# A macaron block on one core: one batch of weighted sums per sequence, a fourth buffer of exponentials, feed-forward products in place

## The chip, the cores and the metric

The kernel runs on one core of a Trainium2 chip. The metric is the device time of one execution in microseconds (us). The core's engines run side by side: PE (TensorE, matrix products, with its weight loads shown as PEld), DVE (VectorE), ACT (ScalarE), POOL (GpSimd) and SP (SyncE, which issues most transfers).

## The reference, cut to what matters

Sixteen sequences of 256 tokens with 256 features pass through half a feed-forward layer, an attention layer and the same half feed-forward layer again, each behind a layer norm and added to its input.

```python
x = x + 0.5 * ffn(layernorm(x))      # silu(x Wu) * (x Wg), times Wd; 1024 hidden features
x = x + attention(layernorm(x))      # 16 heads of 16, keys and values in 4 groups, causal
x = x + 0.5 * ffn(layernorm(x))      # weights quantised to -s, 0, s with s = mean |W|

# of the attention, per sequence and head
scores = where(causal, -inf, q @ k.T / sqrt(16))
attn = softmax(scores, axis=-1)      # over the keys
out = attn @ v                       # the sums over the keys
```

## The kernel before, in words

The 16 sequences are handled in eight blocks n of two (512 tokens). The feed-forward layer is cut into *units*: a unit (ffn_unit, L464) makes 128 of the 1024 hidden features for a block, by four matmuls u and four g of 512 columns (products, L448), and each block has eight units per pass, so that there are 128 in all. After a unit ACT makes th of the u product and DVE makes h: for the first four keys of `order` (SILU = 4) with a Silu and one DVE product (L480, L481), for the other twelve with a Tanh (L483), a DVE product th+1 times u into a tile tmp (L485) and a DVE product with g (L486). ACT then rounds h to 16 bits (L491) and POOL keeps the remainder (L492). Four ffn_down steps (L496) take the products back to 256 features by 16 matmuls d each (L502), and DVE adds them to x (L507).

Before that the three weight matrices are quantised at the start: ternary_sums (L277) adds up absolute values on ACT, with the mapped values going to a tile junk that nothing reads, and on DVE; ternary_piece (L312) then makes each quarter of a matrix in two steps, a tile dn (values under the lower bound; on ACT, DVE or POOL) and the DVE product of L321 that reads dn and writes tu, tg or td.

The attention of sequence q (n, s = divmod(q, 2)) goes through these steps: project and values (queries, keys, values of the block, matmuls qkv), load (transfers of Qs and ks), peak and peak_parts (largest score of each row, DVE L625 and L635 to L646), peak_rows (transposes pt, ACT copy, and a transfer into Qs), exponents, weighted and attended:

- exponents(q, g), L663: for group g three score matmuls st of 512 columns (L675), three ACT exponentials into a tile pT (L676), and two POOL selects that put zeros above the diagonal (L684; issued one step later).
- weighted(q, gp), L693: for the two groups 2gp and 2gp+1 the sums over the keys. Each matmul (L706) has 128 keys and 32 columns of weights (16 values and a one for the denominator) and writes a quarter of the partitions, so four heads' matmuls stand side by side in the array. A first half of the keys goes with 256 query columns, the second with 128. Each group has a PSUM bank of its own, half used, and ACT copies each group's [128, 256] into a tile oT (L713). There are 16 matmul calls in a weighted; the profile shows each as two instructions, since the numbers are 32-bit, so 32 for a call.
- attended(q, gp), L716: four transposes ot, a reciprocal and a product on DVE, and an addition to x on POOL (L733).

Tiles come from pools with a number of slots per tag: pT has 3 slots, oT 3, tmp 3 (the products of L485 and the dn pieces), th 3 (th and junk), and PSUM has 8 banks. A tile that finds no free slot waits until a former one's last reader is done.

Three things set the order of the work. A planner in the kernel (Step, run) issues steps from six chains: the feed-forward chain, and the chains of the norms, loads, sequences, peaks and projections. A step has a cost in planner's microseconds and lags after earlier steps: weighted costs 1.64 and follows LAG_PROB = 3.0 after the second exponents it needs, attended 1.2 after weighted. The sequence chain issues one sequence's steps as e0, e1, e2, w0, e3, a0, w1, a1, with the next sequence's e0 put ahead of w1 (L881 to L888). Attention steps that are due go first, as long as they are not ahead of the feed-forward chain by PACE. The tile library then orders each engine's instructions by its own simulated timeline (L1098); pin (L223) keeps a batch's matmuls in their written order among themselves.

Steps that wait for exponentials by name: load(q) for exponents(q-3, 3) (L839), peak(q, 0) for exponents(q-2, 3) (L849), and the attention's norm of block n for weighted(2(n-3)+1, 1) (L822).

Of the kernel before, what the change touches and what calls it, by code (L numbers as in the profile page):

```python
# [97 lines left out]
def macaron_kernel(  # L98
# [83 lines left out]
    wg = raw[1].rearrange("p (c f) -> p c f", c=EC)  # L182
    wd = raw[2].rearrange("p (c e) -> p c e", c=FC)
    QS = [r.bitcast(F16).rearrange("p (t h q) -> p t h q", t=2, h=H) for r in raw]
    wqkv = ap_.tile([P, 3, 512], F32, tag="pT", name="wqkv", bufs=3)[:, :EC, : 3 * P]

    def load_x(n):
        nc.sync.dma_start(xs[n], x_t[n])
# [49 lines left out]
    def constant_rows():  # L238


        c = ap_.tile([P, 2, 1536], F16, tag="pT", name="constant_rows", bufs=3)
        k, v = c[:, 0, : 3 * S], c[:, 1, :P]
        nc.gpsimd.memset(k[KP:KR], 0.0)
        ku = k[KP:KR].rearrange("p (v u k) -> p v u k", v=3, k=U)
        for which, base in ((EVEN, 0), (ODD, 32)):
            nc.gpsimd.affine_select(
                out=ku[:, which], in_=ku[:, which], pattern=[[0, S // U], [-1, U]],
                compare_op=ALU.is_ge, fill=-MASK, base=base, channel_multiplier=1,
            )
        nc.gpsimd.memset(k[KR : KR + 3], -MROW)  # L250
        nc.gpsimd.memset(v[KP:KR], 0.0)
        vj = v[KP:KR].rearrange("p (j b) -> p j b", b=4)
        nc.gpsimd.affine_select(
            out=vj, in_=vj, pattern=[[1, 32], [0, 4]], compare_op=ALU.not_equal,
            fill=MASK, base=0, channel_multiplier=-1,
        )
        for to in Ks:
            nc.sync.dma_start(
                to[KP : KR + 3].rearrange("p g v k -> p g (v k)"),
                k[KP : KR + 3].unsqueeze(1).to_broadcast([KR + 3 - KP, G, 3 * S]),  # L260
            )
        box["queries"] = v
# [48 lines left out]

    def ternary_piece(wi, ti, hi, lo, name):  # L312
        engine = {"u": ENG_U, "g": ENG_G, "d": ENG_D}[name[0]][int(name[1])]
        dn = fp.tile([P] + list(wi.shape[1:]), BF16, tag="tmp", name=f"dn_{name}")
        if engine == "a":
            nc.scalar.activation(dn, wi, AF.Relu, bias=lo, scale=-1.0)
            nc.scalar.activation(dn, dn, AF.Sign)
        else:
            by = nc.gpsimd if engine == "p" else nc.vector
            pin(PINT and engine == "v", by.tensor_scalar(dn, wi, lo, None, ALU.is_lt))  # L320
        nc.vector.scalar_tensor_tensor(ti, wi, hi, dn, ALU.is_gt, ALU.subtract)  # L321
# [142 lines left out]
    def ffn_unit(key, f):  # L464
        n, p = key
        name = f"{p}_{n}_{f}"
        if f == 0:
            hidden[key] = hp.tile([P, FC, 2, 512], F16, tag="hT", name=f"hT_{p}_{n}")
        hT = hidden[key]
        if (key, f) not in half_done:  # L470
            ffn_up(key, f)
        up = half_done.pop((key, f))
        gate = bank([P, 512], f"g_{name}")
        if key == order[0] and f < 6:
            warm(int(NWF[f]), f"g{f}")
        products(key, f, tg, gate)
        th = fp.tile([P, 512], F32, tag="th", name=f"th_{name}")
        h = fp.tile([P, 512], F32, tag="h", name=f"h_{name}")
        if key in order[:SILU]:
            nc.scalar.activation(th, up, AF.Silu, scale=scales["one_u"])  # L480
            nc.vector.scalar_tensor_tensor(h, gate, scales["per_u"], th, ALU.mult, ALU.mult)  # L481
        else:
            nc.scalar.activation(th, up, AF.Tanh, scale=scales["half_u"])  # L483
            tmp = fp.tile([P, 512], F32, tag="tmp", name=f"tmp_{name}")
            nc.vector.scalar_tensor_tensor(tmp, th, 1.0, up, ALU.add, ALU.mult)  # L485
            nc.vector.scalar_tensor_tensor(  # L486
                h, gate, 0.25 / (NORM * NORM), tmp, ALU.mult, ALU.mult
            )

        def split():  # L490
            nc.scalar.copy(hT[:, f, 0, :], h)  # L491
            nc.gpsimd.tensor_tensor(hT[:, f, 1, :], h, hT[:, f, 0, :], ALU.subtract)  # L492

        later(1, urgent(HP_FFN, split))
# [168 lines left out]
    def exponents(q, g):  # L663
        n, s = divmod(q, 2)
        Qs, ks = made[n][s], Ks[q % NBUF]
        pT = ap_.tile([P, 3, 512], F32, tag="pT", name=f"pT_{q}_{g}", bufs=3)
        probs[q, g] = pT
        every = slice(0, KR + 3)
        for u in range(3):
            sc = bank([P, 512], f"st_{q}_{g}_{u}")  # L670
            if u < 2:
                keys, mov = ks[every, g, PLAIN, 0:P], Qs[every, u, 4 * g : 4 * g + 4, :]
            else:
                keys, mov = ks[every, g, PLAIN, P:], Qs[every, 1, 4 * g : 4 * g + 4, :]
            nc.tensor.matmul(sc, keys, mov, start=True, stop=True)  # L675
            nc.scalar.activation(  # L676
                pT[:, u, :].rearrange("p (h b j) -> p h b j", h=4, b=4),
                sc.rearrange("p (h j b) -> p h b j", h=4, b=4), AF.Exp, scale=exp_scale,
            )

        def causal():
            for u in (0, 2):
                v = pT[:, u, :].rearrange("p (h t) -> p h t", h=4)
                nc.gpsimd.affine_select(  # L684
                    out=v, in_=v, pattern=[[0, 4], [1, P]], compare_op=ALU.is_ge,
                    fill=0.0, base=0, channel_multiplier=-1,
                )

        later(1, urgent(HP_CAUSAL, causal))

    sums = {}

    def weighted(q, gp):  # L693

        n, s = divmod(q, 2)
        v = VT[n % NVAL]
        groups = (2 * gp, 2 * gp + 1)
        pT = [probs.pop((q, g)) for g in groups]
        o = [bank([P, S], f"o_{q}_{g}") for g in groups]
        first = True  # L700
        for half in range(2):
            for i2, g in enumerate(groups):
                for i in range(4):
                    at = o[i2][32 * i : 32 * i + 32]
                    moving = pT[i2][:, 2 * half : 2, i * P : (i + 1) * P] if half == 0 else pT[i2][:, 2, i * P : (i + 1) * P]
                    pin(not first, nc.tensor.matmul(  # L706
                        at[:, half * P :], v[:, 2 * s + half, g, :], moving,
                        start=half == 0, stop=half == 1, tile_position=(0, 32 * i),
                    ))
                    first = False  # L710
        for i2, g in enumerate(groups):
            oT = ap_.tile([P, S], F32, tag="oT", name=f"oT_{q}_{g}", bufs=3)
            nc.scalar.copy(oT, o[i2])  # L713
            sums[q, g] = oT

    def attended(q, gp):  # L716
        n, s = divmod(q, 2)
        ot = bank([P, 2, 2 * P], f"ot_{q}_{gp}").rearrange("p b (h d) -> p b h d", d=32)
        for gg in range(2):
            oT = sums.pop((q, 2 * gp + gg))  # L720
            for b in range(2):
                nc.tensor.transpose(  # L722
                    ot[:, b, 4 * gg : 4 * gg + 4, :].rearrange("p h d -> p (h d)"),
                    oT[:, b * P : (b + 1) * P], ident,
                )
        rs = small.tile([P, 2, 8, 1], F32, tag="rs", name=f"rs_{q}_{gp}")
        nc.vector.reciprocal(rs, ot[:, :, :, D : D + 1])
# [83 lines left out]
    def qkv_chain():  # L811
        steps = []
        for n in range(NSB):
# [5 lines left out]
            if n > 1:  # L819
                need.append((("load", 2 * n - 3), 0.0))  # L820
            if n >= NVAL:
                need.append((("weighted", 2 * (n - NVAL) + 1, 1), 0.0))  # L822
            at = 8 * n - QKV_LEAD
            if at >= 0:
                need.append((("exponents", at // 4, at % 4), 0.0))
# [36 lines left out]
    def sequence_chain():  # L862
        steps = []
        for q in range(2 * NSB):
            e = [
                Step(0.66, lambda q=q, g=g: exponents(q, g), ("exponents", q, g),
                     [(("exponents", q, g - 1), GAP_EXP)] if g else
                     [(("rows", q), LAG_MAX), (("values", q // 2), 0.0)])
                for g in range(4)
            ]  # L870
            w = [
                Step(1.64, lambda q=q, gp=gp: weighted(q, gp), ("weighted", q, gp),
                     [(("exponents", q, 2 * gp + 1), LAG_PROB)])
                for gp in range(2)
            ]
            a = [
                Step(0.43, lambda q=q, h=h: attended(q, h), ("attended", q, h),
                     [(("weighted", q, h), 1.2)])
                for h in range(2)
            ]  # L880
            steps.append([e[0], e[1], e[2], w[0], e[3], a[0], w[1], a[1]])  # L881
        flat = []
        for q, mine in enumerate(steps):
            flat += mine

        for q in range(1, 2 * NSB):
            i = 8 * q
            flat[i - 2 : i + 1] = [flat[i], flat[i - 2], flat[i - 1]]  # L888
        return flat

# [211 lines left out]
```

## Time and profile before

| | |
|---|---|
| three runs, median | 563.08 us (561.78 to 563.2) |
| the profiled execution, its own time | 560.4 us |
| its span, first to last instruction | 558.7 us |
| mean granted clock of TensorE | 0.991 |
| weighted sums, matmuls o (L706) | 1024 instructions, 49.4 us busy |
| copies of the sums (L713) | 64 of 128x256, 388 ns each |
| exponentials (L676) | 192, 697 ns each |
| selects (L684) | 128, 636 ns each |
| th (L483), its product (L485), h (L486) | 96 each, 692, 683 and 685 ns |

The profile is of one execution. "Busy" is the time in which at least one instruction of a group ran on its engine; a matmul's end is modelled, so matmuls in a row overlap by their records, and the distance of two starts says more than a duration. In a list of groups, `out<-in` gives the tiles by the program's names, then partitions x elements, and the idle time of the engine in front with what ended it. In a timeline neighbouring instructions of a kind are merged, with their number behind x. In a list of waits the three numbers are the sum, how often, and the longest.

### The profile page before, as it was taken

The page shows a single profiled execution, that of the slowest core. Times are in us where ns is not written, and L with a number is a line of the kernel's source. Part 1 is how long each engine was busy: PE and PEld are TensorE (multiplying, and loading weights), DVE is VectorE, ACT ScalarE, POOL GpSimd, SP SyncE. Part 2 cuts the span into 40 slices and gives each one's busy share as a digit, 9 for nine tenths or more (in the row PEclk, how much of TensorE's full clock was granted, in tenths as well). Part 3 has the DMA queues.
Part 4 walks back from the last instruction along what each step waited for, and adds up shares of the span by engine and source line. Part 5 has one row for each costly group of instructions (what it writes and reads, how often), then busy time and mean ns, then how long its engine had stood idle before and what let it go on. Part 6 is the DMA issues. An engine that isn't in the chain of part 4 may idle for free.

```text
span 558.7 us, 12132 instructions
## 1 busy us (share of the span) xinstructions
PE 537.8 (96%) x4593; PEld 330.6 (59%) x4593; DVE 433.1 (78%) x1027; ACT 376.0 (67%) x658; POOL 355.0 (64%) x380
## 2 busy tenths in 40 slices
PE   5999999989999999999999998999999999999997
PEld 5546556647556665665665664566645576565565
DVE  5988989978889899869777887459955697847653
ACT  5796757496688678677766749755698445874642
POOL 4367787675589568577745539854589534865542
PEclk8899999999999999999999999999999999999999
DMA  8933288561077068058249003572024930020201
GB/s 293 299 48 57 39 207 128 161 124 31 12 185 111 1 163 144 4 152 147 27 126 163 1 3 39 144 162 40 1 40 74 207 79 22 12 68 11 67 28 49
DMA packets 119317, 51.25 MB, mean 92 GB/s; under 512 B 85174, under 2 KB 119002, under 8 KB 119258
## 3 DMA queue, kind: packets, MB, share of 16 engines
q1 hardware_dynamic: 118825, 50.08, 40.8%
q8 instruction: 36, 0.59, 0.4%
q10 hardware_dynamic: 432, 0.39, 0.3%
q14 instruction: 24, 0.19, 0.1%
HBM read 22.41 MB, written 14.68 MB: 66 GB/s over the span
## 4 chain that ended last, share of the span: by engine, by line
PE 72%; DVE 11%; ACT 7%; DMA 5%; POOL 3%; issue 2%; SPq 0%; DVEq 0%; ACTq 0%; POOLq 0%
PE d L502 18%; PE u L451 15%; PE g L451 15%; PE o L706 6%; PE s L611 6%; PE st L675 5%; PE qkv L525 4%; DMA Qs<-prows 2%; ACT pT L676 2%; PE ot L722 2%; DVE tops L625 2%; DVE h L486 1%; DVE tmp L485 1%; DMA xT_a<-xparts_a 1%; DVE xn_f L352 1%
## 5 line engine op out<-in xcount | busy, mean ns | idle before, releaser
L492 POOL TENSOR_TENSOR hT<-h,hT 128x512 f16<-128x512 f32 x128 | 149.0, 1169 | 88.0 <-ACT hT L491 87.1
L676 ACT ACTIVATE pT<-st,exp_scale 128x512 f32<-128x512 f32 x192 | 119.8, 697 | 26.3 <-PE st L675 26.2
L502 PE MATMUL d<-td,hT 128*128 128x256 f16 x1024 | 122.5, 273 | 0.2 <-ACT pT L676 0.2
L491 ACT CAST hT<-h 128x512 f16<-128x512 f32 x128 | 79.5, 621 | 56.0 <-DVE h L486 40.9
L625 DVE TENSOR_REDUCE tops<-s 128x8 f32<-128x512 f32 x160 | 103.0, 677 | 16.3 <-PE s L611 15.9
L451 PE MATMUL u<-xT_f,tu 128*128 128x512 f16 x448 | 115.3, 379 | 0.3 <-DVE h L486 0.3
L684 POOL TENSOR_SCALAR_AFFINE_SELECT pT<-pT 128x512 f32<-128x512 f32 x128 | 80.4, 636 | 55.3 <-ACT pT L676 52.9
L451 PE MATMUL g<-xT_f,tg 128*128 128x512 f16 x448 | 115.3, 379 | 0.0
L502 PEld LDWEIGHTS <-hT 128*128 128x128 f16 x1024 | 98.5, 98 | 18.2 <-issue 0.5
L485 DVE SCALAR_TENSOR_TENSOR tmp<-th,u 128x512 f32<-128x512 f32 x96 | 65.5, 683 | 50.4 <-ACT th L483 49.9
L483 ACT ACTIVATE th<-u,half_u 128x512 f32<-128x512 f32 x96 | 66.2, 692 | 42.8 <-PE u L451 42.4
L451 PEld LDWEIGHTS <-tg 128*128 128x128 f16 x512 | 49.9, 98 | 62.0 <-DVE tg L321 2.0
L451 PEld LDWEIGHTS <-tu 128*128 128x128 f16 x512 | 47.2, 99 | 43.1 <-issue 2.0
L486 DVE SCALAR_TENSOR_TENSOR h<-g,tmp 128x512 f32<-128x512 f32 x96 | 65.6, 685 | 5.4
L675 PE MATMUL st<-Qs,ks 99*128 99x512 f16 x192 | 54.1, 380 | 6.3 <-DMA Qs<-prows 3.0
L611 PEld LDWEIGHTS <-Qs 96*128 96x128 f16 x896 | 50.9, 116 | 12.7 <-issue 3.0
L611 PE MATMUL s<-ks,Qs 96*128 96x64 f16 (+2 forms) x896 | 53.4, 208 | 0.0
L706 PE MATMUL o<-pT,vt 128*32 128x128 f32 (+1 forms) x1024 | 49.4, 329 | 0.0
L706 PEld LDWEIGHTS o<-pT,vt 128*32 128x32 f32 x1024 | 28.4, 109 | 25.2 <-issue 8.3
L507 DVE SCALAR_TENSOR_TENSOR x<-d,so,x 128x256 f32<-128x256 f32 x64 | 30.4, 477 | 14.1 <-PE d L502 13.6
L525 PE MATMUL qkv<-xT_a,wparts 128*128 128x512 f16 x144 | 34.6, 379 | 1.9 <-DMA xT_a<-xparts_a 1.9
L367 POOL TENSOR_TENSOR xparts_f<-xn_f,xparts_f 128x1024 f16<-128x1024 f32 x14 | 29.8, 2131 | 10.2 <-ACT xparts_f L364 8.2
(163 smaller groups left out, 603.2 us busy)
## 6 DMA issues: line engine op xcount, KB each, us to landing
qd<-sp SPq DMA_DIRECT2D x32, 256.0 KB, 2.6
Qs<-qd SPq DMA_DIRECT2D x64, 128.0 KB, 3.5
ks<-kd SPq DMA_DIRECT2D x48, 128.0 KB, 3.6
x<-in_x SPq DMA_DIRECT2D x8, 512.0 KB, 8.7
out<-x SPq DMA_DIRECT2D x32, 128.0 KB, 3.1
kd<-sp SPq DMA_DIRECT2D x16, 128.0 KB, 2.4
Qs<-in_w_upT SPq DMA_DIRECT2D x4, 256.0 KB, 5.5
Qs<-in_w_gateT SPq DMA_DIRECT2D x1, 1024.0 KB
```

The lines of the kernel that those rows point to most:

```text
L451: nc.tensor.matmul(acc, w[:, c, f * P : (f + 1) * P], ffn_ready[key][:, a, c, :], start=(c == 0 and a == 0), stop=(c == EC - 1 and a == 1),)
L485: nc.vector.scalar_tensor_tensor(tmp, th, 1.0, up, ALU.add, ALU.mult)
L486: nc.vector.scalar_tensor_tensor(h, gate, 0.25 / (NORM * NORM), tmp, ALU.mult, ALU.mult)
L491: nc.scalar.copy(hT[:, f, 0, :], h)
L492: nc.gpsimd.tensor_tensor(hT[:, f, 1, :], h, hT[:, f, 0, :], ALU.subtract)
L502: nc.tensor.matmul(acc, hT[:, f, a, t * P : (t + 1) * P], td[:, f, :], start=(f == 0 and a == 0), stop=(f == FC - 1 and a == 1),)
L611: nc.tensor.matmul(sc[:, at : at + n, :], Qs[0:KR, b // 4, g * P : (g + 1) * P, b % 4], k[:, g, which, first * U : (first + n) * U], start ...
L625: nc.vector.tensor_reduce(peaks[q][:, u, :], sc, AX.X, ALU.max)
L675: nc.tensor.matmul(sc, keys, mov, start=True, stop=True)
L676: nc.scalar.activation(pT[:, u, :].rearrange("p (h b j) -> p h b j", h=4, b=4), sc.rearrange("p (h j b) -> p h b j", h=4, b=4), AF.Exp, sc ...
L684: nc.gpsimd.affine_select(out=v, in_=v, pattern=[[0, 4], [1, P]], compare_op=ALU.is_ge, fill=0.0, base=0, channel_multiplier=-1,)
L706: pin(not first, nc.tensor.matmul(at[:, half * P :], v[:, 2 * s + half, g, :], moving, start=half == 0, stop=half == 1, tile_position=(0, ...
```

## The change

weighted(q) now handles all four groups of a sequence in one call. Its matmuls are the same in number and size, in another order: groups 0 and 2 with both halves of the keys, then 1 and 3. Two groups share a PSUM bank, so that two banks are used in full, and two copies of [128, 512] replace four of [128, 256]; oT has two slots of twice the size. pT has four slots. The sequence chain is e0, e1, e2, e3, w, a0, a1 with the next e0 ahead of a0; w costs 2.9 in the planner, and the second attended has a lag of 1.6. The product of L485 is written over th; the tag tmp is gone, and the dn pieces of the quantisation take their slots from th's three.

```diff
-        dn = fp.tile([P] + list(wi.shape[1:]), BF16, tag="tmp", name=f"dn_{name}")
+        dn = fp.tile([P] + list(wi.shape[1:]), BF16, tag="th", name=f"dn_{name}")
...
-            tmp = fp.tile([P, 512], F32, tag="tmp", name=f"tmp_{name}")
-            nc.vector.scalar_tensor_tensor(tmp, th, 1.0, up, ALU.add, ALU.mult)
+            nc.vector.scalar_tensor_tensor(th, th, 1.0, up, ALU.add, ALU.mult)
             nc.vector.scalar_tensor_tensor(
-                h, gate, 0.25 / (NORM * NORM), tmp, ALU.mult, ALU.mult
+                h, gate, 0.25 / (NORM * NORM), th, ALU.mult, ALU.mult
             )
...
-        pT = ap_.tile([P, 3, 512], F32, tag="pT", name=f"pT_{q}_{g}", bufs=3)
+        pT = ap_.tile([P, 3, 512], F32, tag="pT", name=f"pT_{q}_{g}", bufs=4)
...
-    def weighted(q, gp):
+    def weighted(q):
...
-        for half in range(2):
-            for i2, g in enumerate(groups):
-                for i in range(4):
...
+        for i2 in range(2):
+            for half in range(2):
+                for gp in range(2):
+                    g = 2 * gp + i2
+                    for i in range(4):
+                        cut = slice(i * P, (i + 1) * P)
+                        moving = pT[g][:, 0:2, cut] if half == 0 else pT[g][:, 2, cut]
+                        pin(not first, nc.tensor.matmul(
+                            o[gp][32 * i : 32 * i + 32, i2, half * P :], v[:, 2 * s + half, g, :], moving,
+                            start=half == 0, stop=half == 1, tile_position=(0, 32 * i),
+                        ))
+                        first = False
+        for gp in range(2):
+            oT = ap_.tile([P, 2, S], F32, tag="oT", name=f"oT_{q}_{gp}", bufs=2)
+            nc.scalar.copy(oT, o[gp])
+            sums[q, gp] = oT
...
-                need.append((("weighted", 2 * (n - NVAL) + 1, 1), 0.0))
+                need.append((("weighted", 2 * (n - NVAL) + 1), 0.0))
...
-            steps.append([e[0], e[1], e[2], w[0], e[3], a[0], w[1], a[1]])
+            w = Step(2.9, lambda q=q: weighted(q), ("weighted", q), [(("exponents", q, 3), LAG_PROB)])
...
+                Step(0.43, lambda q=q, h=h: attended(q, h), ("attended", q, h), [(("weighted", q), 1.2 + 0.4 * h)])
...
+            steps.append(e + [w] + a)
```

More of the change, by code (lines that the diff above doesn't have):

```diff
@@ L184, in macaron_kernel @@
     QS = [r.bitcast(F16).rearrange("p (t h q) -> p t h q", t=2, h=H) for r in raw]
-    wqkv = ap_.tile([P, 3, 512], F32, tag="pT", name="wqkv", bufs=3)[:, :EC, : 3 * P]
+    wqkv = ap_.tile([P, 3, 512], F32, tag="pT", name="wqkv", bufs=4)[:, :EC, : 3 * P]
     def load_x(n):
@@ L238, in constant_rows @@
     def constant_rows():
-        c = ap_.tile([P, 2, 1536], F16, tag="pT", name="constant_rows", bufs=3)
+        c = ap_.tile([P, 2, 1536], F16, tag="pT", name="constant_rows", bufs=4)
         k, v = c[:, 0, : 3 * S], c[:, 1, :P]
@@ L691, in macaron_kernel @@
     sums = {}
-    def weighted(q, gp):
+    def weighted(q):
         n, s = divmod(q, 2)
         v = VT[n % NVAL]
-        groups = (2 * gp, 2 * gp + 1)
-        pT = [probs.pop((q, g)) for g in groups]
-        o = [bank([P, S], f"o_{q}_{g}") for g in groups]
+        pT = [probs.pop((q, g)) for g in range(G)]
+        o = [bank([P, 2, S], f"o_{q}_{gp}") for gp in range(2)]
         first = True
-        for half in range(2):
-            for i2, g in enumerate(groups):
-                for i in range(4):
[L704 to L714, printed above, removed]
+        for i2 in range(2):
[14 more added lines that the diff above has]
+            sums[q, gp] = oT
     def attended(q, gp):
@@ L718, in attended @@
         ot = bank([P, 2, 2 * P], f"ot_{q}_{gp}").rearrange("p b (h d) -> p b h d", d=32)
+        oT = sums.pop((q, gp))
         for gg in range(2):
-            oT = sums.pop((q, 2 * gp + gg))
             for b in range(2):
@@ L723, in attended @@
                     ot[:, b, 4 * gg : 4 * gg + 4, :].rearrange("p h d -> p (h d)"),
-                    oT[:, b * P : (b + 1) * P], ident,
+                    oT[:, gg, b * P : (b + 1) * P], ident,
                 )
@@ L870, in sequence_chain @@
             ]
[L871 to L875, printed above, removed]
+            w = Step(2.9, lambda q=q: weighted(q), ("weighted", q), [(("exponents", q, 3), LAG_PROB)])
             a = [
-                Step(0.43, lambda q=q, h=h: attended(q, h), ("attended", q, h),
-                     [(("weighted", q, h), 1.2)])
+                Step(0.43, lambda q=q, h=h: attended(q, h), ("attended", q, h), [(("weighted", q), 1.2 + 0.4 * h)])
                 for h in range(2)
             ]
-            steps.append([e[0], e[1], e[2], w[0], e[3], a[0], w[1], a[1]])
+            steps.append(e + [w] + a)
         flat = []
@@ L886, in sequence_chain @@
         for q in range(1, 2 * NSB):
-            i = 8 * q
+            i = 7 * q
             flat[i - 2 : i + 1] = [flat[i], flat[i - 2], flat[i - 1]]
```

## Prediction

> **What bounds the kernel now.** I read the page first, then the table by stage, the waits of PE, and PE's own timeline around the batches that the change rebuilds.
>
> From the page, busy times and the 40 slices:
>
> ```profile
> PE 537.8 (96%) x4593; PEld 330.6 (59%) x4593; DVE 433.1 (78%) x1027; ACT 376.0 (67%) x658; POOL 355.0 (64%) x380
> PE   5999999989999999999999998999999999999997
> ```
>
> The matmul row is full from the second slice to the last but one; the other engines have a fifth of the span or more to spare. PE stands idle for 558.7 − 537.8 = 20.9 us. The table by stage (columns: stretch, busy us and count of each engine, clock, DMA) says where:
>
> ```profile
> 0.00:25.00 25.00, 17.98 (x79) 12.73 (x80) 19.22 (x65) 15.16 (x29) 9.03 (x23) 0.80 0.96 313
> 25.00:110.00 85.00, 84.69 (x567) 50.43 (x566) 75.54 (x180) 57.76 (x97) 62.71 (x49) 1.00 0.53 104
> 110.00:310.00 200.00, 194.22 (x1929) 119.08 (x1928) 164.93 (x389) 147.66 (x263) 135.78 (x154) 1.00 0.48 100
> 310.00:505.00 195.00, 190.61 (x1694) 116.15 (x1693) 142.30 (x340) 131.84 (x232) 122.91 (x133) 1.00 0.30 64
> 505.00:558.00 53.00, 50.29 (x330) 32.19 (x328) 31.09 (x56) 23.58 (x39) 24.59 (x21) 1.00 0.15 41
> ```
>
> 7.0 us of the idle time lie in the start, 5.8 and 4.4 us in the two attention stages (110 to 505), the rest at the end. So this is a kernel whose matmuls set the time, and a microsecond of PE work removed is a microsecond gained, unless a new wait takes its place.
>
> A page of the Trainium skill speaks against reading the 96% like that: "Trainium Kernel Development and Optimization", Performance Expectations, says that matmul busy time is a bad metric for the distance to roofline, because matmuls are pipelined, and points to the weight loads' share instead. By that rule PE, at 59%, would have room and the change would gain about nothing; by the starts in the timeline below, where matmuls follow each other without a gap, it gains what it removes. I go by the starts.
>
> PE's timeline (start, modelled duration, line, count):
>
> ```profile
> 199.70 1.51 PE L706 MATMUL o<-pT,vt 128*32 128x256 f32 x32
> 201.14 0.66 PE L611 MATMUL s<-ks,Qs 96*128 96x192 f16 x10
> ...
> 205.85 1.03 PE L451 MATMUL g<-xT_f,tg 128*128 128x512 f16 x4
> 206.72 0.81 PE L675 MATMUL st<-Qs,ks 99*128 99x512 f16 x3
> 207.37 1.03 PE L451 MATMUL u<-xT_f,tu 128*128 128x512 f16 x4
> 208.23 1.03 PE L451 MATMUL g<-xT_f,tg 128*128 128x512 f16 x4
> 209.19 1.29 PE L706 MATMUL o<-pT,vt 128*32 128x256 f32 x24
> 210.41 0.82 PE L675 MATMUL st<-Qs,ks 99*128 99x512 f16 x3
> 211.16 0.35 PE L654 MATMUL pt<-identh,pparts 128*24 128x128 f16 x3
> 211.29 0.31 PE L706 MATMUL o<-pT,vt 128*32 128x128 f32 x3
> ```
>
> The reader should use starts, not durations. An undisturbed batch of 32 (one call of weighted) takes 201.14 − 199.70 = 1.44 us; its first 24 take 210.41 − 209.19 = 1.22, so the last eight, two sets of four side by side at 128 columns, cost 0.22, or 0.11 a set. A set at 256 columns is then 0.22, and the eight sets of a batch need 4 x 0.22 + 4 x 0.11 = 1.32. The remaining **0.12 us** are filling and emptying. And a batch costs its neighbour: four g matmuls take 206.72 − 205.85 = 0.87 before an ordinary successor, 209.19 − 208.23 = 0.96 before a batch: **0.09 us** on entry. Each entry into such a batch and exit from it thus costs 0.21 us of PE, whatever is in it. The second fence shows more: this batch is cut, and other work runs between its pieces. PE's timeline has five batches cut after 24 instructions (159.3, 209.2, 246.3, 269.6, 423.5), and this one's rest is cut once more: 38 entries for 32 calls.
>
> **The change part by part.**
>
> *One call instead of two.* The 1024 matmul instructions stay, with the same columns; their sets only come in another order. 16 of the 32 forced entries go: 16 x 0.21 = −3.4 us, all of it on PE and so on the path. The six cuts cost 6 x 0.21 = 1.3 us now; with half as many calls I take half of it as gone, −0.6 (bounds 0 and −1.3; a longer call could also be cut more often). Sum on PE: −4.0.
>
> *Copies of the sums.* 64 copies of 128x256 at 388 ns (22.5 us busy) become 32 of 128x512. No such copy is in the trace; the nearest rows of that shape are the hT cast, 621 ns, and the exponential from PSUM, 697 ns: 19.9 to 22.3 us. The gain of 0 to 2.6 us is ACT's, which has 180 us idle: nothing. The transposes behind them (L722) wait for a copy that is 0.25 to 0.3 us longer; the next sequence's first scores (0.65 us of PE) and a feed-forward unit (1.73) lie between by the planner's lags of 1.2 and 1.6. Without that cover it is 0.3 us for each of 32 transposing steps, some 9 us; today PE waits for such a copy 0.2 us in all.
>
> *All four exponentials before the sums.* The fourth buffer lets exponents(q, 3) run without waiting for sums to free one, and what hangs on it (load of q+3, first peaks of q+2) can start earlier. PE's waits name what could profit or suffer:
>
> ```profile
> PE st L675 <- DMA Qs<-prows: 3.0, 4, 1.1
> PE st L675 <- ACT pT L676: 2.0, 2, 1.4
> PE qkv L525 <- DMA xT_a<-xparts_a: 1.9, 1, 1.9
> PE pt L654 <- DVE pparts L646: 1.3, 1, 1.3
> ```
>
> These 8.2 us are accidents of the order (four, two, one and one occurrences in 16 sequences). The new order deals them anew; I take 0, with −4 and +4 as bounds, half of the pot either way. The planner's cost for the sums falls from 3.28 to 2.9 a sequence, which shifts the interleaving slightly; that is in the same bound. No DMA is added or removed, none is moved by itself.
>
> *Products in place.* The same two DVE instructions a unit (683 and 685 ns). The in-place form that the trace has is L507, 477 ns at 256 columns, with which nothing as wide compares; the nearest wide scalar-tensor-tensor is L481's 740. So between nothing and 57 ns x 96 = 5.5 us of DVE, which is 78% busy; I take nothing, since two operands and one result stay what they were. The th slot is held about 0.7 us longer, until L486 ends; three slots serve units that come every 558.7/128 = 4.4 us on average. ACT's tanh would wait for the slot, and exponentials behind it, if DVE fell some 3 us behind.
>
> *The ternary pieces move to the th slots.* This is the price of the change. Six slots (three tmp, three th) become three for the junk of the sums, the dn pieces and the first th. In the trace dn pieces already queue: the GpSimd piece waits 2.0 us for a DVE product (L321). From the timelines of ACT and DVE between 16.75 and 30.2 I add up how long each is held: dn about 24.6 us (for one, dn of the second gate column from 16.75 to 23.4), th 12.6, junk 2.2: 39.4 us against 3 x 13.4 = 40.2 that three slots have. That does not pack without delay. Slack stands against it for the columns: the third gate piece is done at 24.2 and its matmuls start at 26.95, the fourth at 27.7 against 31.4. For the rows there is none: the last td piece ends at 44.34 (DVE's timeline) and the first tile's d matmuls, stopped at 44.33, go on at 44.44. I take delays of 2 to 4 us, mostly covered by slack and by u and g matmuls in front: **+1.2 us**, bounds 0 and +4.
>
> *Sum.* −3.4 − 0.6 + 1.2 = −2.8 us. The profiled execution took 560.4 us (span 558.7 and 1.7 around it), so 557.6. The median of the three runs shown is 563.08, 0.5% above the profiled one; carried over to it, 563.08 − 2.8 = **560.3 us**. Everything below is on that footing.
>
> **The rivals.**
>
> *It doesn't do what it says, or the time comes back.* A batch of 64 is cut as often as two of 32 (22 or more entries left), or the engines behind PE, starved for 2.6 us in place of 1.3, hand the time back: DVE is at 82% in the stage 110 to 310. For: the cuts of today. Against: PE's waits for DVE in that stage are under 2 us. About 563, chance 0.15.
>
> *The start pays more.* Slots delay the row pieces by 4 us and nothing covers it: −4.0 + 4 = 0, 563.1. For: the sum above fills the slots, and td ends just in time. Against: other units' matmuls can be put in front. 0.06.
>
> *The stalls go too.* The earlier fourth exponent brings peaks and rows forward; half of the 8.2 us goes, and all cuts: −3.4 − 1.3 − 4 + 0 = −8.7, 554.4. Against: rows wait for DVE and a DMA as well. 0.12.
>
> *Slower: PE waits in front of each batch.* It now needs the selects of four groups at once, the last of them behind three exponentials (0.70 each) and two selects (0.64 each) of exponents(q, 3), on a POOL queue where the subtraction of L492 (1.17) may stand ahead. Place: before L706, 16 times. Price: at 0.5 us each 8 us, so −2.8 + 8 = +5.2, **568.3**. It decides from 0.28 us a batch, where 16 x 0.28 = 2.8 + 1.7. For: there's no second, earlier half batch any more, and the first sequence stalls for exponentials already (1.4 and 0.5 us). Against: today weight loads of batches wait for selects six times, 2.1 us in all, PE itself never, and the lag of 3.0 is kept. 0.17.
>
> **How the numbers follow.** The forecast has 0.50. Below 0.3% (1.7 us) this kernel can't be told from no change. Faster: forecast and stalls gone, 0.62; within: first and second rival, 0.21; slower: 0.17. The range goes from 554 to 568.5: the low case, and the slower one at its price.
>
> **What would show it.** Right: 16 runs of o with 64 instructions, 2.6 + 0.12 us from start to next start, at most three cuts, PE's busy time 3 to 4 us lower, and idle time as before but for a microsecond at the start. The last td piece done at 45 to 47 instead of 44.3. Wrong: PE waits for selects at L706 or for copies at L722 of more than 3 us together; a start in which the first d matmuls come over 2 us later; cuts above six; or the idle time of 110 to 505 over 14 us instead of 10.2.

## The result and the profile after

The changed kernel takes 566.35 us (median of 7 runs, 564.79 to 568.74) against 561.83 us for the kernel before (7 runs, 560.49 to 563.22): a ratio of 1.0084, 95% interval 1.0062 to 1.0106. It is slower by 0.84%, where the forecast had it faster. The profiled execution took 566.3 us with a span of 564.6, 5.9 us above the profiled one of before.

First the page's busy times and slices of the changed kernel:

```profile
PE 536.0 (95%) x4593; PEld 334.0 (59%) x4593; DVE 434.5 (77%) x1027; ACT 375.2 (66%) x626; POOL 353.5 (63%) x380
PE   5999789999999998999899999999889999999997
...
PEclk8799979999999999999999999999999999999999
```

PE is busy for 1.8 us less and idle for 28.6 us instead of 20.9. The dent is in the fifth slice, and a slice later the granted clock, which was full from the third slice on before, falls once more. The table by stage of the changed kernel, in the columns used for the kernel before:

```profile
0.00:25.00 25.00, 18.25 (x79) 13.14 (x80) 18.84 (x64) 15.02 (x28) 8.97 (x24) 0.80 0.96 312
25.00:110.00 85.00, 79.10 (x492) 45.30 (x491) 68.00 (x165) 55.07 (x92) 58.65 (x46) 0.96 0.46 86
110.00:310.00 200.00, 193.45 (x1890) 121.22 (x1888) 162.81 (x386) 144.57 (x243) 134.16 (x150) 1.00 0.47 103
310.00:505.00 195.00, 189.00 (x1774) 118.72 (x1773) 149.51 (x351) 134.95 (x225) 125.40 (x140) 1.00 0.31 68
505.00:564.50 59.50, 56.21 (x367) 35.66 (x365) 35.38 (x64) 25.58 (x41) 26.31 (x23) 1.00 0.14 41
```

The loss lies between 25 and 110 us, before the first sequence reaches its sums: 75 matmul instructions fewer than before have started by 110 us (492 against 567), and PE is idle for 5.9 us where it was idle for 0.3. The waits of PE name it:

```profile
PE qkv L524 <- DMA xT_a<-xparts_a: 7.0, 2, 5.3
PE pt L653 <- DVE pparts L645: 2.9, 2, 2.2
PE st L674 <- ACT pT L675: 1.9, 2, 1.4
PE st L674 <- DMA Qs<-prows: 1.8, 1, 1.8
```

PE's timeline of the changed kernel around it:

```profile
65.04 1.91 PE L501 MATMUL d<-td,hT 128*128 128x256 f16 x16
72.26 6.81 PE L524 MATMUL qkv<-xT_a,wparts 128*128 128x512 f16 x18 [5.32 <-DMA xT_a<-xparts_a]
79.01 0.46 PE L572 MATMUL v<-ident,full 64*128 64x64 f32 x4
```

and the same place in the kernel before:

```profile
64.36 1.91 PE L502 MATMUL d<-td,hT 128*128 128x256 f16 x16
66.11 4.05 PE L525 MATMUL qkv<-xT_a,wparts 128*128 128x512 f16 x18
70.09 0.46 PE L573 MATMUL v<-ident,full 64*128 64x64 f32 x4
```

Eighteen projection matmuls of the first block stand still for 5.3 us, for the transfer that transposes the block's norm, and then need 79.01 − 72.26 = 6.75 us instead of 3.98: after the pause they run at half pace. Wait and half pace are 8.1 us. The first score matmul st starts at 119.36 us instead of 110.64, 8.7 us later; from there to the end of the span it is 445.2 us instead of 448.0, **2.8 us less**. The change thus gains 2.8 of the 4.0 us forecast for the batches behind the first st and loses three times that in front.

The batches themselves are as forecast. PE's timeline of the changed kernel:

```profile
134.59 1.03 PE L451 MATMUL g<-xT_f,tg 128*128 128x512 f16 x4
135.54 2.81 PE L706 MATMUL o<-pT,vt 128*32 128x256 f32 x64
138.28 0.82 PE L674 MATMUL st<-Qs,ks 99*128 99x512 f16 x3
```

64 instructions from start to next start take 2.74 us (worked out: 2.76), and the 16 calls are entered 19 times, with three cuts.

### The profile page after: what moved, and what is told of

It reads as the page before. It is cut to its first block, busy times and chain, and to the rows that moved or that the text cites. A ratio compares the mean times of both kernels' runs of the same rounds, so it can differ in the third digit from the quotient of the medians.

```text
span 564.6 us, 12015 instructions
## 1 busy us (share of the span) xinstructions
PE 536.0 (95%) x4593; PEld 334.0 (59%) x4593; DVE 434.5 (77%) x1027; ACT 375.2 (66%) x626; POOL 353.5 (63%) x380
## 4 chain that ended last, share of the span: by engine, by line
PE 65%; DVE 15%; ACT 6%; issue 4%; POOL 3%; DMA 3%; POOLq 0%; DVEq 0%; ACTq 0%
PE d L501 16%; PE u L451 13%; PE g L451 13%; PE o L706 6%; PE st L674 5%; PE s L610 4%; PE qkv L524 4%; DVE tops L624 3%; ACT pT L675 2%; DVE h L485 2%; PE ot L722 2%; DMA xT_a<-xparts_a 2%; DVE th L484 1%; DVE xn_f L352 1%; DVE st_f L332 1%
## 5 line engine op out<-in xcount | busy, mean ns | idle before, releaser
L675 ACT ACTIVATE pT<-st,exp_scale 128x512 f32<-128x512 f32 x192 | 120.5, 706 | 20.4 <-PE st L674 19.9
L501 PEld LDWEIGHTS <-hT 128*128 128x128 f16 x1024 | 98.4, 98 | 19.9 <-issue 1.0
L484 DVE SCALAR_TENSOR_TENSOR th<-th,u 128x512 f32<-128x512 f32 x96 | 65.4, 682 | 36.7 <-ACT th L483 36.5
L485 DVE SCALAR_TENSOR_TENSOR h<-g,th 128x512 f32<-128x512 f32 x96 | 65.9, 686 | 5.9 <-PE st L674 0.5
L706 PE MATMUL o<-pT,vt 128*32 128x128 f32 (+1 forms) x1024 | 45.5, 328 | 0.0
L524 PE MATMUL qkv<-xT_a,wparts 128*128 128x512 f16 x144 | 36.3, 402 | 7.5 <-DMA xT_a<-xparts_a 7.0
L554 POOL TENSOR_TENSOR sp<-full,sp 128x512 f16<-128x512 f32 (+1 forms) x24 | 27.8, 1161 | 22.8 <-DVE sp L549 22.8
```

Of the source, the lines that this page charges most:

```text
L484: nc.vector.scalar_tensor_tensor(th, th, 1.0, up, ALU.add, ALU.mult)
L485: nc.vector.scalar_tensor_tensor(h, gate, 0.25 / (NORM * NORM), th, ALU.mult, ALU.mult)
L501: nc.tensor.matmul(acc, hT[:, f, a, t * P : (t + 1) * P], td[:, f, :], start=(f == 0 and a == 0), stop=(f == FC - 1 and a == 1),)
L675: nc.scalar.activation(pT[:, u, :].rearrange("p (h b j) -> p h b j", h=4, b=4), sc.rearrange("p (h j b) -> p h b j", h=4, b=4), AF.Exp, sc ...
L706: pin(not first, nc.tensor.matmul(o[gp][32 * i : 32 * i + 32, i2, half * P :], v[:, 2 * s + half, g, :], moving, start=half == 0, stop=hal ...
```

## The experiments

Theory A: the dn pieces in th's slots delay the quantised rows, these the first block's sums and norm, and so the transfer; PE waits and loses its clock. Theory B: the wait comes from the order that the new batch and its planner cost give. Each kernel was timed beside the kernel before on one chip. "First st" is the start of the first score matmul in the profiled execution, "rest" the span minus that; both are of one execution per kernel. The intervals in the text are 95% intervals of the ratio to the kernel before.

| kernel | first st, us | rest, us |
|---|---|---|
| before | 110.6 | 448.0 |
| after (the change) | 119.4 | 445.2 |
| e1: change, dn in own memory | 110.9 | 444.5 |
| e2: before, dn in th's slots | 118.2 | 450.0 |
| e3: before, products in place | 110.1 | 449.6 |
| e4: change, projections later | 121.4 | 439.5 |
| e5: change, row pieces in own memory | 112.1 | 446.1 |
| e6: change, column pieces in own memory | 112.7 | 446.0 |
| e7: change, dn in six own places | 114.8 | 448.2 |
| e8: change, matmuls in the wait | 117.3 | 445.6 |
| e9: e5 and e4 | 120.2 | 440.5 |
| e10: before, projections later | 120.2 | 455.5 |
| e11: change, weights' split a step later | 112.0 | 444.6 |

### dn in memory of its own

```diff
-        dn = fp.tile([P] + list(wi.shape[1:]), BF16, tag="th", name=f"dn_{name}")
+        if "dn" not in box:
+            box["dn"], box["pieces"] = ap_.tile([P, 3, 1024], BF16, tag="pT", name="dn", bufs=4), 0
+        dn = box["dn"][:, box["pieces"] % 3, :512].rearrange("p (a b) -> p a b", a=2)
+        box["pieces"] += 1
```

> The changed kernel, but the dn pieces of the quantisation live in memory of their own again (three places in a tile lent from the fourth exponentials' slot, which is unused until 113 us). In the changed kernel PE waits 5.3 us at 72 us for the first block's transposed norm, and the next 13 projection matmuls start 0.42 us apart instead of 0.21 (2.8 us). Theory A (shared slots delay the quantised rows, these the first d matmuls' sums, the norm and the transfer): both go, the last td piece is done before 45 us, time 566.4 - 8 = 558 us. Theory B (the wait comes from the order that the new batch and its planner cost give, not from slots): the wait stays, 565 to 567 us.

Measured: 560.85 us, ratio 0.9972 (0.9947 to 0.9997). The wait at the first projections is gone, they run from 66.5 to 70.1, the last td piece ends at 44.6 (43.66 + 0.96), and the first st is back at 110.9. The median is 5.5 us below the changed kernel's, not 8. The start isn't what is missing: although it has a wait of its own (2.7 us for a sum of absolute values on DVE, 0.7 in the changed kernel's place), its first st is 8.4 us earlier than the changed kernel's. The profiled execution, 557.1 us, is the fastest of ten and 3.75 us below their median; why the others take longer isn't shown. What follows: with everything else of the change kept, the loss in front of the first st goes.

### dn in th's slots, alone

```diff
-        dn = fp.tile([P] + list(wi.shape[1:]), BF16, tag="tmp", name=f"dn_{name}")
+        dn = fp.tile([P] + list(wi.shape[1:]), BF16, tag="th", name=f"dn_{name}")
```

> The kernel before, with the one edit that dn takes its slots from th's; tmp and two batches stay. Theory A: the wait for the first block's norm appears here too, 561.8 + 8 = 570 us (566 at least). Theory B: no wait at the projections, 561 to 563 us.

Measured: 567.96 us, ratio 1.0095 (1.0064 to 1.0126). PE's timeline of this kernel:

```profile
64.77 1.91 PE L502 MATMUL d<-td,hT 128*128 128x256 f16 x16
71.83 6.07 PE L525 MATMUL qkv<-xT_a,wparts 128*128 128x512 f16 x18 [5.15 <-DMA xT_a<-xparts_a]
77.84 0.46 PE L573 MATMUL v<-ident,full 64*128 64x64 f32 x4
```

The same stall at the same place, in a kernel with two batches, tmp and the old planner. Theory B has fallen: one word of the diff, the tag, costs 5.4 us between medians (567.96 against 562.53 beside it), more than the change loses as a whole.

### Products in place, alone

The edit is that of L485 and L486 in the change.

> The kernel before, with the one edit that the product of L485 is written over th; dn keeps the tmp slots. Both theories: within 1.5 us of 561.8, no wait over 2 us at the first projections; DVE's two products stay at 0.68 us each. If holding th longer costs something, it shows as ACT waiting in front of its tanh and a time above 564.

Measured: 562.14 us, ratio 0.9991 (0.9972 to 1.0009). No difference, as both theories had it. Against e1, which adds the batch of four groups, its median is 1.3 us higher; in the table the parts of the spans behind the first st differ by 5.2 us. The three kernels with two batches and the old lag have 448.0, 449.6 and 450.0 there, the six with one batch and that lag 444.5, 444.6, 445.2, 445.6, 446.0 and 446.1, and e7 448.2. Means of 449.2 and 445.8 (e7 counted): the new order is worth 3.5 us in the profiled executions. They flatter it, since e1's and e11's are the fastest of ten; an estimate that puts each kernel's median in place of its profiled time and leaves the first st where it is gives 449.3 and 446.5, so 2.7 us. No run has the batch without the fourth buffer and the new planner costs, so this is their joint worth.

### The projections held back

```diff
-LAG_NORM0 = 10.0
+LAG_NORM0 = 14.0
```

> The changed kernel with the planner's lag of the first block's projections after its norm raised from 10 to 14, so that about two more units of PE work stand in front of them. Both theories: the wait of 5.3 us falls under 1 us, the following matmuls keep 0.21 us from start to start, time 558 to 560 us. If 566 stays with the wait gone, the wait was not what the change costs, and some later stall takes its place.

Measured: 562.68 us, ratio 1.0009 (0.9991 to 1.0027). The first projections run at full pace now, 0.21 us apart, but the wait moved: it stands at the next block's projections (4.1 us, at 98 us). The part behind the first st is shorter by another 6 us, which neither theory had. The expectation held for the place and failed for the sum.

### Rows or columns

Both take the edit of the first experiment under a condition, `name[0] == "d"` here and `name[0] != "d"` in the other.

> The changed kernel, with the dn pieces of the row matrix alone (four of twelve) in memory of their own; the column pieces stay in th's slots. If the late rows are what delays the first block's norm (td's last piece ends at 47.5 us in the changed kernel, 44.3 before): the wait at the first projections goes and the time is as with all dn apart, 560 to 562 us. If the loss starts with the column pieces (16 to 31 us), the wait stays: 565 to 567.

Measured: 558.2 us, ratio 0.9927 (0.9902 to 0.9952), the fastest kernel of the study and 1.8 us under the lower of the two ranges; PE doesn't wait at the first projections.

> The changed kernel, with the dn pieces of the two column matrices (eight of twelve) in memory of their own; the row pieces stay in th's slots. The mirror of the run before: if the rows matter, 565 to 567 us with the wait of over 4 us at the first projections; if the columns matter, 560 to 562.

Measured: 560.51 us, ratio 0.9984 (0.9951 to 1.0018), with 0.7 us of wait at the first projections. The two sides of this pair were expected to differ in the stall, and they don't: taking either group out of th's slots is enough to remove the stall. The row pieces alone in these slots don't bring it: in this run the last td piece still ends late, at 46.4 us, but on ACT the norm's rounding (L370, 59.39) stays ahead of the weights' scaling (L1026, 60.34). The last experiment tests that order.

### Six places

```diff
+            box["dn"], box["pieces"] = ap_.tile([P, 6, 512], BF16, tag="pT", name="dn", bufs=4), 0
+        dn = box["dn"][:, box["pieces"] % 6, :512].rearrange("p (a b) -> p a b", a=2)
```

> The changed kernel with all dn pieces in memory of their own, six places in place of three. If slots still bind with three, the start gets shorter by up to 2 us against that kernel, 559 us; if three are enough, the same within 1.5 us, 559.5 to 562.5. In both cases no wait at the first projections beyond 1 us.

Measured: 564.2 us, ratio 1.0027 (1.0005 to 1.0049): slower than with three places, against both expectations. More room let three dn_u pieces and two tu products run on DVE ahead of part_g, the sum that the second matrix's scale s_g needs, and two more tu products ahead of s_g itself: it comes at 20.34 us, against 16.93 with three places (e1). The wait at the first projections is gone, as expected. PE's waits of this kernel:

```profile
PE g L454 <- DVE tg L324: 3.6, 1, 3.6
PE allsum_g L301 <- DVE part_g L293: 3.4, 1, 3.4
```

Three slots were not only a shortage; they also held less urgent pieces back.

### Matmuls in the wait

```diff
+        if n == 0 and j == 2:
+            warm(26, "projections")
         ps = bank([P, 512], f"qkv_{n}_{j}")
```

> The changed kernel with 26 added matmuls on constants directly in front of the first block's projections (5.7 us of PE work that nothing reads), so that PE does not stand still while it waits for the transposed norm. If the halved pace of the 13 projection matmuls after the wait (2.8 us) comes from PE having stood idle, they run 0.21 us apart and the time falls by 2 to 3 us, to 563.5 us, though the wait for the transfer is as long. If the pace has another cause, nothing changes or the added work costs: 566 to 569.

Measured: 564.82 us, ratio 1.0044 (1.0015 to 1.0072). PE's timeline of this kernel:

```profile
66.87 5.97 PE L219 MATMUL warm_projections<-ones 128*128 128x128 f32 x52
73.00 4.05 PE L526 MATMUL qkv<-xT_a,wparts 128*128 128x512 f16 x18 [0.16 <-DMA xT_a<-xparts_a]
76.98 0.46 PE L574 MATMUL v<-ident,full 64*128 64x64 f32 x4
```

The transfer is as late, yet the projections take 3.98 us again: the half pace after the gap came from PE's standing still. The first st comes 2.1 us earlier than in the changed kernel (117.3). The time falls by less than the 2 to 3 us expected: 1.5 us from median to median, or 0.4% from ratio to ratio, with intervals that overlap.

### Both repairs, and the lag alone

> The changed kernel with the row pieces in memory of their own and the first block's projections held back as well (lag 14). With the rows apart the start took 112.1 us up to the first score matmul and 442.4 from there; with the late projections alone it was 121.4 and 435.8. If the shorter second part came from the later start of attention (its waits re-dealt), it comes here too and the time is 552 to 556 us; if it came from the late norm itself, the second part is 441 or more and the time 557 to 561.

Measured: 563.03 us, ratio 1.0012 (0.9985 to 1.0039). The expectation counts the second part up to the start of the last matmul; so counted it is 436.8 us here, as short as with the late projections alone (by the table's count 440.5 against 439.5). The first is long again (120.2), with 4.0 us of wait at the second block's projections: neither of the two outcomes expected.

> The kernel before with that lag alone raised from 10 to 14. In the kernel before the transposed norm lands at 64.9 us and the projections' weights are ready at 65.4, and PE comes to them at 66.1, so nothing is waited for at the start and a later place gains nothing there: 560 to 564 us. If the lag by itself re-deals the later waits for the better, 555 to 559; it would then owe nothing to the batch of four groups.

Measured: 576.17 us, ratio 1.0249 (1.0181 to 1.0318), also outside both. In the kernel before the later projections make both parts longer, by 9.5 us up to the first st and by 7.4 behind it. PE's waits of it:

```profile
PE qkv L525 <- DMA xT_a<-xparts_a: 7.8, 2, 4.8
PE pt L654 <- DVE pparts L646: 6.0, 4, 2.7
```

So the shorter second part of e4 and e9 is no effect of the lag alone; why batch and lag together give it stays open. It doesn't touch the cause of the loss.

### The weights' split a step later

```diff
-        (16, constant_queries), (PM + 11, projections_split), (KM, constant_rows), ...
+        (16, constant_queries), (PM + 12, projections_split), (KM, constant_rows), ...
```

> The changed kernel, dn still in th's slots, with projections_split (the scaling and splitting of the projections' weights) issued one feed-forward step later. In the changed kernel its instructions stand ahead of the first block's norm on ACT (L1020 before L364) and POOL (L1022 before L367), in the kernel before behind them; one step later they are behind again. If the late rows cost as much as they do because they let the weights' split pass the norm, xparts_a is done by 64 us instead of 67.7, the wait at the projections falls from 5.3 us to 2 at most (then for the weights), and the time to 559 to 562 us. If the delay of the rows alone makes the wait, it stays above 3 us and the time at 564 to 567.

This run asks how three late microseconds become seven. POOL's timeline of the kernel before:

```profile
58.50 2.13 POOL L367 TENSOR_TENSOR xparts_a<-xn_a,xparts_a 128x1024 f16<-128x1024 f32 x1
...
63.35 2.07 POOL L1027 TENSOR_TENSOR wparts<-wqkv,wparts 128x768 f16<-128x768 f32 x1 [1.61 <-DVE wparts L1026]
```

of the changed kernel, dn in th's slots:

```profile
62.81 1.65 POOL L1022 TENSOR_TENSOR wparts<-wqkv,wparts 128x768 f16<-128x768 f32 x1 [2.04 <-DVE wparts L1021]
64.41 1.17 POOL L491 TENSOR_TENSOR hT<-h,hT 128x512 f16<-128x512 f32 x1
65.52 2.14 POOL L367 TENSOR_TENSOR xparts_a<-xn_a,xparts_a 128x1024 f16<-128x1024 f32 x1
```

of the kernel with the split a step later:

```profile
60.99 2.13 POOL L367 TENSOR_TENSOR xparts_a<-xn_a,xparts_a 128x1024 f16<-128x1024 f32 x1
64.72 1.65 POOL L1022 TENSOR_TENSOR wparts<-wqkv,wparts 128x768 f16<-128x768 f32 x1 [1.61 <-DVE wparts L1021]
```

Measured: 562.09 us, ratio 1.0008 (0.9986 to 1.0031). xparts_a is done at 63.1, PE waits 1.37 us, the projections run at full pace, and the first st comes at 112.0. The last td piece still ends late (46.7). The median stands 0.1 us above the upper end of what was expected; the profiled execution (558.3) is the fastest of ten. The mechanism is as expected: the late rows cost so much because, with them, the weights' split stands ahead of the norm in two queues.

## Why the prediction was wrong

**The batch: right.** −3.4 for the entries and −0.6 for half of the cuts; 38 entries became 19, 19 x 0.21 = 4.0 us, and the busy time of o fell from 49.4 to 45.5. PE's busy time as a whole fell by 1.8 us and not by the 3 to 4 that were named, since the slow projections add 1.7 (qkv 36.3 against 34.6). Behind the first st the kernels with one batch are 3.5 us shorter on average in the profiled executions, 2.7 by the estimate from the medians. The reading by weight loads would have had nothing; that most of PE's 4.0 us counts is borne out, that all of it does is not shown.

**Copies and products in place: right.** The 32 copies of 128x512 take 585 ns, 17.5 us in all, below the bounds of 19.9 to 22.3, and nobody waits longer for them; e3 shows the products at nothing, with DVE at 683 and 684 ns (682 and 686 in the changed kernel).

**The slower rival: wrong mechanism.** PE never waits for a select in front of a batch. The chance for slower, 0.17, was placed on a place where nothing happened; that 566.35 lies near its price of 568.3, and so under the top of the range, is luck. The rival that named the start had a chance of 0.06 and ended at 563.1, no change.

**The ternary pieces: the step that failed.** The prediction put it as "+1.2 us, bounds 0 and +4", with the remark that the rows had no slack. What was looked at were the d matmuls themselves, and there the estimate was nearly right: the last td piece ends at 47.5 instead of 44.3 (45 to 47 was named), the first d matmuls start at 43.69 instead of 43.02, and PE runs on with 52 of them from 45.11, before the last piece is done. What was not followed is who waits for the d matmuls' results. DVE's timeline of the kernel before:

```profile
43.37 0.97 DVE L321 SCALAR_TENSOR_TENSOR td<-Qs,hi_d,dn_d 128x512 f16<-128x512 f32 x1
...
47.18 0.48 DVE L507 SCALAR_TENSOR_TENSOR x<-d,so,x 128x256 f32<-128x256 f32 x1
...
52.48 0.17 DVE L336 TENSOR_SCALAR ve_a<-mv_a 128x4 f32<-128x4 f32 x1
```

and of the changed kernel:

```profile
46.76 0.73 DVE L321 SCALAR_TENSOR_TENSOR td<-Qs,hi_d,dn_d 128x512 f16<-128x512 f32 x1
...
49.46 0.92 DVE L506 SCALAR_TENSOR_TENSOR x<-d,so,x 128x256 f32<-128x256 f32 x2 [0.27 <-PE d L501]
...
56.26 0.16 DVE L336 TENSOR_SCALAR ve_a<-mv_a 128x4 f32<-128x4 f32 x1
```

In the kernel before the chain runs like this: x of the first tiles at 47.2, the norm's xn_a at 53.9, its rounding on ACT at 57.2, xparts_a on POOL at 58.5 to 60.6, the transposing transfer from 60.7, landed at 64.9; the projections' weights are done at 65.4, and PE gets to the projections at 66.1. **The slack of this chain was 0.7 to 1.2 us** (1.2 for the norm, 0.7 for the weights), and no view in the prediction showed it, since a wait that just doesn't happen is in no list of waits. In the changed kernel x comes at 49.5, 2.3 us late, and xn_a at 58.1: the norm is 4.2 us late. The other 1.9 us are DVE's own order, in which feed-forward products (L481, 53.70 and 54.83) and steps of the weights' scaling (L1005 to L1007) now stand ahead of ve_a. Then ACT's queue has the weights ahead. Its timeline, before and changed:

```profile
57.21 1.04 ACT L364 CAST xparts_a<-xn_a 128x1024 f16<-128x1024 f32 x1
...
60.69 1.30 ACT L1025 ACTIVATE wqkv<-wqkv,up 128x512 f32<-128x512 f32 x3 [0.82 <-DVE up L1021]
```

```profile
58.57 1.08 ACT L347 ACTIVATE xn_a<-x,shift_a,rstd_a 128x256 f32<-128x256 f32 x2
60.83 1.30 ACT L1020 ACTIVATE wqkv<-wqkv,up 128x512 f32<-128x512 f32 x3 [1.18 <-DVE up L1016]
...
63.12 1.04 ACT L364 CAST xparts_a<-xn_a 128x1024 f16<-128x1024 f32 x1
```

Before, the rounding was done (57.2 to 58.3) when the weights came (60.7). On POOL it is the same with L1022. Both add 2.8 us, the transfer starts 7.0 us late (67.7) and lands at 72.0. PE, with as much work in front of the projections as before (23.1 us from the first d matmul, 23.2 now), waits 5.3 us, and the pause costs 2.8 us more through the clock: 0.7 + 5.3 + 2.8 = 8.8 us, and 8.7 measured at the first st, against +1.2. In the profiled executions +8.7 − 2.8 = +5.9 us thus stands where the prediction had +1.2 − 4.0 = −2.8.

Shown by experiment: the tag alone makes the loss (e2), its removal takes it away (e1, e5, e6), the half pace comes from the pause (e8), and the place of the weights' split makes the larger part of the wait (e11, where 1.4 us are left of 5.3). Argued only: that exactly the slots, and not the order that the library derived from having fewer of them, make the rows late; on the chip the two can't be parted, since the order is fixed when the program is built.

**The waits of the new order: inside their bounds.** Behind the first st the new order brings a wait of 2.2 us for pparts in front of pt that the kernel before didn't have, and 1.8 of the 3.0 us for prows stay; e1, e5 to e8 and e11 share the wait for pparts to a tenth. PE's idle time from 110 to 505 us is 12.6 us instead of 10.2. Set at 0 with −4 and +4, which holds. The sum's footing of 563.08 us, a median of three runs, was 1.25 us above that of seven, 561.83.

A version that keeps the gain without the loss is e5: the batch, with the row pieces out of th's slots, 0.73% faster than before.

## What to carry to other kernels

When a change delays something, follow it to the end of its chain of waiters, across every queue that it stands in, and compare when it arrives with when it is used; the slack of a wait that isn't there shows only in that comparison. Where the order of the queues is fixed when the program is built, as here, a delay of a few microseconds can put another chain ahead, and is then paid a second time. Sharing slots between a startup phase and the steady state is a change of the startup's order, and neither fewer nor more slots are safe without looking at what runs first.

## What the runs showed of the hardware that had not been expected

A pause of PE is paid beyond its length. After 5.3 us of standing still the next 13 matmuls of 512 columns started 0.43 us apart instead of 0.21, 2.8 us in all, and not after the same stretch filled with useless matmuls. The page "TensorE: Matmul & The Clock Gate" of the Trainium skill, section "Why this matters for your kernels", warns of gaps of over some 3 us; the 5.3 us agree. So do the other waits of 3.9 us and more behind 60 us: 5.15 in e2, 4.09 in e4, 3.95 in e9 and 4.78 in e10 all have projection matmuls at half pace behind them. But half pace also comes after a shorter wait. In e1, PE's timeline shows a wait of 1.44 us and then u and g groups that need 1.69 and 1.56 us (from start to next start) instead of 0.87:

```profile
116.12 0.59 PE L677 MATMUL st<-Qs,ks 99*128 99x512 f16 x2 [1.44 <-ACT pT L678]
116.70 0.83 PE L613 MATMUL s<-ks,Qs 96*128 96x64 f16 x16
117.34 1.90 PE L454 MATMUL u<-xT_f,tu 128*128 128x512 f16 x4
119.03 1.72 PE L454 MATMUL g<-xT_f,tg 128*128 128x512 f16 x4
120.59 0.81 PE L677 MATMUL st<-Qs,ks 99*128 99x512 f16 x3
```

Ten of the kernels have this wait, of 1.39 to 1.44 us, at their first exponentials. Behind it, matmuls run at half pace in the profiles of e1, e3, e7, e8 and e11, and at full pace in those of the kernel before, the changed one, e2, e5 and e6. So whether such a pause costs some 1.5 us more is not settled by its length alone. This may be a part of why runs of one kernel here spread by 7 us and more: e6's fastest run, 558.4 us, has a mean granted clock of 0.991, its slowest, 565.94 us, one of 0.981. That the pauses are the reason is not shown, and in e4 and e7 the clock doesn't follow the time.
